# Loading the adjacency of blocks 4 to 15 two blocks at a time in a graph-attention kernel

## The chip, the cores and the metric

The kernel runs on one core of one Trainium2 chip. The metric is the device time of one execution in microseconds; the value of a kernel is the median of its runs. Lower is better.

## The reference, cut to what matters

The reference is one graph-attention layer with a residual and a layer norm. `x` is 4096 x 512, `adj` 4096 x 4096, `W` 512 x 2048 (four heads side by side), all float32.

```python
ht = (h @ W).reshape(N, N_HEADS, N_HIDDEN).transpose(1, 0, 2)
src = einsum('hnd,hd->hn', ht, a_src); dst = einsum('hnd,hd->hn', ht, a_dst)
e = leaky_relu(src[:, :, None] + dst[:, None, :], SLOPE) + adj_mat[None]
att = softmax(e, axis=-1)
h_prime = einsum('hij,hjd->hid', att, ht)
out = layernorm(x + h_prime.mean(axis=0))
```

`adj` holds values up to 1e9, so in each row the largest entry normally outweighs everything else: the attention is then a one at one column, and `h_prime.mean` is the row of `x` at that column times the mean of the heads of `W`. The kernel computes this leading case, tests it with a bound, and has a general branch for blocks in which the test fails. The inputs here stay in the leading case, so the work below is the whole time.

## The kernel before, in words

Rows are taken in 32 blocks of 128: partition p of block ib is row 32p + ib, so consecutive blocks lie side by side in memory on each partition. One block of `adj` is 128 x 4096 float32, 2048 KB, which is 16 KB in a piece on each partition. A core must read all 64 MB of it, besides `x`, `W` and a row of `x` gathered per output row, and it must write 8 MB.

`leading_rows` is one loop over t = 0 to 31, with the order on every engine written out by hand (`manual_schedule`). The engines work on different blocks at the same t:

- **SP** issues all large transfers, in program order. `load_adj` (L119 to L124) loads block t + 5 into one of six buffers; it has to wait until the buffer's last block has been reduced. Blocks from 28 on come in two or four pieces. `load_x` (L127) loads rows of `x` into `hold`, in which part of the rows first hold `W` (`load_w`, L130). After the loop come the stores of `hold` (L338).
- **DVE** reduces block t to maxima of segments of 16, 32 or 64 columns (`segment_maxima`, L180), finds the largest one and its place (`find_segment`, L187 and L189).
- **POOL** fetches that segment out of `adj` again by an indirect DMA (`fetch_segment`, tile `lead`, L200). Two steps later `find_column` (L217, L223) finds the column inside it, and POOL gathers the row of `x` at that column (`gather_rows`, tile `y`, L211). The last block takes another way: `find_column_in_row` (L231) searches the whole row.
- **PE** turns the gathered rows of block t - 3 (`turn`, L238; ACT copies the result, L240), adds the rows of `x` by an identity product (`residual`, L246) and multiplies by the mean of the heads (`products`, L253; halves in L295). In steps 1 to 14 it also turns `W` for the bound (`turn_w`, `head_vector`).
- **ACT and POOL** do the statistics and the scaling of blocks t - 4 and t - 6 (`stats`, `rstd`, `finish`).

The distances are set in the line `COLUMN, PROJECT, STATS, FINISH = 2, 3, 4, 6`. Results are kept in `hold` and stored after the loop, as SP reads its queue in order: first blocks 0 to 7 by four, then 8 to 15 by two, then 16 to 23 by four, then the last eight as they become ready.

A transfer gets one of eight semaphores in turn, and waits for the transfer that had it before.

Of the kernel before, what the change touches and what calls it, by code (L numbers as in the profile page):

```python
# [9 lines left out]
F32 = mybir.dt.float32  # L10
# [10 lines left out]
P = 128  # L21
# [49 lines left out]
def leading_rows(ctx, tc, x, adj, W, a, out, ident, v, n_bad, any_bad):  # L71
# [8 lines left out]
    nc = tc.nc  # L80
    N, D = x.shape
    H = a.shape[0]
    KB, NB = D // P, N // P
    AHEAD = 5
    Q = 4
    PIECES = 4
    LATE = NB - Q
    BEHIND = LATE - Q

    once = ctx.enter_context(tc.tile_pool(name="once", bufs=1))  # L90
    adj_pool = ctx.enter_context(tc.tile_pool(name="adj_pool", bufs=AHEAD + 1))
    y_pool = ctx.enter_context(tc.tile_pool(name="y_pool", bufs=4))
    lead_pool = ctx.enter_context(tc.tile_pool(name="lead_pool", bufs=1))
    LEADS = (8, 8, LAST)
# [3 lines left out]

    adj_rows = adj.rearrange("(p nb) m -> nb p m", nb=NB)
    spans = ((E_EARLY, 0, EARLY), (E, EARLY, NB - LAST), (E_LAST, NB - LAST, NB))  # L100
    adj_segs = {e: adj.rearrange("n (s e) -> (n s) e", e=e) for e, _, _ in spans}
    x_rows = x.rearrange("(p nb) d -> p nb d", nb=NB)
    out_rows = out.rearrange("(p nb) d -> p nb d", nb=NB)
# [1 line left out]


    once.tile([P, 24], F32, name="pad")
    hold = once.tile([P, NB, D], F32, name="hold")
    w_at = NB - KB * H
    w_sum = once.tile([P, KB, D], F32, name="w_sum")  # L110
# [3 lines left out]
    adj_t = {}  # L114

    def pieces(ib):
        return PIECES if ib == NB - 1 else 2 if ib >= LATE else 1

    def load_adj(ib):  # L119
        if 0 <= ib < NB:  # L120
            t = adj_t[ib] = adj_pool.tile([P, N], F32, name="adj_t")
            n = pieces(ib)
            for k in range(n):
                nc.sync.dma_start(t[:, ts(k, N // n)], adj_rows[ib][:, ts(k, N // n)])  # L124

    def load_x(lo, n):
        nc.sync.dma_start(hold[:, ds(lo, n), :], x_rows[:, ds(lo, n), :])  # L127
# [10 lines left out]
    for kb in range(0, KB, 2):  # L138
        load_w(kb, 2)
        load_adj(kb // 2 + 1)  # L140
    for ib in range(KB // 2 + 1, AHEAD):
        load_adj(ib)
    load_x(0, Q)

    make_identity(nc, ident)
# [25 lines left out]
    seg_of, at_of, lead_of, y_t, yt_of, o_ps = {}, {}, {}, {}, {}, {}  # L171
# [13 lines left out]
    def find_segment(ib):  # L185
        seg = seg_of.pop(ib)
        nc.vector.max(out=top[:, ib, :], in_=seg)  # L187
        at = at_of[ib] = small.tile([P, 8], U32, name="at")
        nc.vector.max_index(at, top[:, ib, :], seg)  # L189
        if ib < NB - 1:  # L190
            fetch_segment(ib)
# [17 lines left out]
    def gather_rows(ib, col):  # L209
        y = y_t[ib] = y_pool.tile([P, D], F32, name="y")  # L210
        nc.gpsimd.indirect_dma_start(  # L211
            out=y, out_offset=None, in_=x,
            in_offset=bass.IndirectOffsetOnAxis(ap=col[:, :1], axis=0),
        )

    def find_inner(ib):
        nc.vector.max(out=inner[:, ib, :], in_=lead_of[ib])  # L217

    def find_column(ib):
        if ib < BEHIND:  # L220
            find_inner(ib)
        within = small.tile([P, 8], U32, name="within")
        nc.vector.max_index(within, top[:, ib, :], lead_of[ib])  # L223
        col = small.tile([P, 1], U32, name="col")
        nc.gpsimd.tensor_tensor(col, at_of.pop(ib), within[:, 0:1], op=OP.add)  # L225
        gather_rows(ib, col)
# [7 lines left out]
    def turn(ib):  # L234
        y = y_t.pop(ib)
        tp = psum.tile([P, KB, P], F32, name="tp", bufs=2)
        for kb in range(KB):
            nc.tensor.transpose(tp[:, kb, :], y[:, ds(kb, P, KB)], ident)  # L238
        yt = yt_of[ib] = rows.tile([P, KB, P], F32, name="yt")
        nc.scalar.copy(yt, tp)  # L240

    def residual(ib):
        start = ib not in o_ps
        if start:
            o_ps[ib] = psum.tile([P, D], F32, name="o")
        nc.tensor.matmul(o_ps[ib], ident, hold[:, ib, :], start=start, stop=False)  # L246

    def products(ib, lo=0, hi=KB):
        start = ib not in o_ps
        if start:  # L250
            o_ps[ib] = psum.tile([P, D], F32, name="o")
        for kb in range(lo, hi):
            nc.tensor.matmul(  # L253
                o_ps[ib], yt_of[ib][:, kb, :], w_sum[:, kb, :],
                start=(start and kb == 0), stop=(kb == KB - 1),
            )

    def row_norm(ib):
        sq = rows.tile([P, D], F32, name="sq")
        nc.scalar.activation(sq, hold[:, ib, :], AF.Square, accum_out=xx[:, ib : ib + 1])  # L260

    def put_by(ib):

        if ib == BEHIND:
            o_ps["by"] = adj_pool.tile([P, N // D, D], F32, name="adj_t")
        nc.scalar.copy(o_ps["by"][:, ib - BEHIND, :], o_ps.pop(ib))

    def add_x(engine, ib):
        o = o_ps[ib] = o_ps["by"][:, ib - BEHIND, :]
        engine.tensor_add(o, o, hold[:, ib, :])  # L270

    def stats(ib):
        o, i = o_ps[ib], slice(ib, ib + 1)
        sq = rows.tile([P, D], F32, name="sq")
        nc.scalar.activation(sq, o, AF.Identity, scale=-1.0 / D, accum_out=nm[:, i])  # L275
        sq = rows.tile([P, D], F32, name="sq")
        nc.scalar.activation(sq, o, AF.Square, bias=nm[:, i], accum_out=sd[:, i])  # L277

    def rstd(i):
        nc.gpsimd.tensor_scalar(sd[:, i], sd[:, i], 1.0 / D, EPS, op0=OP.mult, op1=OP.add)  # L280
        nc.gpsimd.tensor_tensor(sd[:, i], sd[:, i], power[:, : i.stop - i.start], op=OP.pow)
        nc.gpsimd.tensor_mul(nm[:, i], nm[:, i], sd[:, i])

    def finish(ib):
        i = slice(ib, ib + 1)
        nc.scalar.activation(hold[:, ib, :], o_ps.pop(ib), AF.Identity, bias=nm[:, i], scale=sd[:, i])  # L286
# [50 lines left out]
    def store(queue, lo, n):  # L337
        queue.dma_start(out_rows[:, ds(lo, n), :], hold[:, ds(lo, n), :])  # L338
# [25 lines left out]
    def head_vector(kb, h, wt):  # L364

        for k in range(KB):
            nc.tensor.matmul(  # L367
                pv[:, kb, h : 2 * H : H], wt[:, k, :], at_d[:, k, h : 2 * H : H],
                start=(k == 0), stop=(k == KB - 1),
            )  # L370
# [57 lines left out]
    vectors = [(kb, h) for kb in range(KB) for h in range(H)]  # L428
    vectors_at = {t: 2 if t < 3 else 1 for t in range(1, 15)}
    COLUMN, PROJECT, STATS, FINISH = 2, 3, 4, 6  # L430

    for t in range(NB):
        if t == NB // 2:
            tc.mark_branch_hint_location("general", engines=HINTED)
        if t in x_at:
            load_x(*x_at[t])
        if t + AHEAD == NB - 1:
            load_x(LATE, Q)
        load_adj(t + AHEAD)
        middle = 1 if t == NB - 1 else 2  # L440
        segment_maxima(t, 0, middle)
        if t >= COLUMN:
            find_column(t - COLUMN)
        segment_maxima(t, middle, PIECES)
        pair = FINISH <= t < BEHIND + FINISH and t % 2 == 0
        if pair:
            rstd(slice(t - FINISH, t - FINISH + 2))
        if t == NB - 1:
            for ib in (BEHIND, BEHIND + 2):
                load_x(ib, 2)  # L450
        find_segment(t)
        if t < 2:
            mean_of_heads(t)
        elif t == 2:
            mean_of_heads(2)
            mean_of_heads(3)
        if t == 0:
            turn_a()
        turned = [(*vectors[0], turn_w(*vectors.pop(0))) for _ in range(vectors_at.get(t, 0))]
        if t == 16:  # L460
            head_norms()
        ib = t - PROJECT
        if t == NB - 1:
            for late in range(LATE, NB):
                row_norm(late)
        if t == NB - 2:
            residual(LATE)
            residual(LATE + 1)
        if ib >= 0:
            turn(ib)  # L470
            if ib > BEHIND:
                products(ib - 1, KB - 1, KB)
            if ib < BEHIND:
                residual(ib)
        for some in turned:
            head_vector(*some)
        if ib >= 0:
            products(ib, 0, KB if ib < BEHIND else KB - 1)
        if t >= BEHIND + STATS:
            put_by(t - STATS)  # L480
        elif t >= STATS:
            stats(t - STATS)
            row_norm(t - STATS)
        if pair:
            finish(t - FINISH)
            finish(t - FINISH + 1)

    for ib in range(BEHIND, LATE):
        row_norm(ib)
    nc.scalar.activation(xx, xx, AF.Sqrt)  # L490
    for ib in range(0, 2 * Q, Q):
        store(nc.sync, ib, Q)
    for ib in range(2 * Q, 4 * Q, 2):
        store(nc.sync, ib, 2)
    for ib in range(4 * Q, BEHIND, Q):
        store(nc.sync, ib, Q)
    add_x(nc.gpsimd, BEHIND)
    find_column(NB - 2)
# [208 lines left out]
```

## Time and profile before

| | us |
|---|---|
| median of 3 runs | 235.0 (234.98 to 235.17) |
| profiled execution, whole | 234.9 |
| its span, first to last instruction | 233.4 |
| around the span | 1.5 |
| DVE busy | 191.3 |
| PE busy | 199.9 |
| queue of SP and ACT transfers, 88.08 MB | 89.1% of 16 engines' span |
| POOL's gathers, 8.84 MB | 9.6% of 16 engines' span |

The span is the profiled execution's own. Engine rows are busy time within it. The two rows on queues give the time that their packets took, divided by the time of all 16 DMA engines.

### The profile page before, as it was taken

To read this page: it belongs to the slowest core of one execution; us is meant where nothing else is said; L and a number is where in the kernel's file an instruction comes from. 1 tells how busy PE (TensorE), PEld (TensorE's weight loads), DVE (VectorE), ACT (ScalarE), POOL (GpSimd) and SP (SyncE) were. 2 spreads that over 40 slices of the span, in tenths; PEclk is the share of its full clock that TensorE was granted. 3 is DMA by queue.
4 is the path that set the end of the run, shared out by engine and by line. 5 is a ranking of instruction groups with operands and counts; after the bars stand their busy time and mean duration, and the time that the engine had idled before them with its cause. 6 is when DMAs were issued, how large, how long until landed. Compare 5 with 4: busy or idle time off the path is not lost.

```text
span 233.4 us, 2484 instructions
## 1 busy us (share of the span) xinstructions
PE 199.9 (86%) x683; PEld 105.3 (45%) x683; DVE 191.3 (82%) x300; ACT 111.8 (48%) x267; POOL 100.7 (43%) x215
## 2 busy tenths in 40 slices
PE   0069995999999999999999779879998977999980
PEld 0034644646565555665645244334443433444460
DVE  0548299689929999999788995999999999998881
ACT  2001223014474757575767455545664644188561
POOL 2020234414524464644543452647464564548300
PEclk9999999579999999999999979999999999999997
DMA  6999999999999999999999999999999999999995
GB/s 237 423 432 428 428 438 426 415 439 436 422 421 437 423 431 425 431 419 428 430 430 428 432 423 432 423 430 421 426 433 420 426 423 426 412 424 420 421 414 213
DMA packets 12257, 97.12 MB, mean 416 GB/s; under 512 B 1992, under 2 KB 2440, under 8 KB 6480
## 3 DMA queue, kind: packets, MB, share of 16 engines
q1 hardware_dynamic: 8640, 88.08, 89.1%
q0 software_dynamic: 3584, 8.84, 9.6%
q8 instruction: 6, 0.10, 0.2%
q14 instruction: 11, 0.09, 0.1%
q10 hardware_dynamic: 16, 0.02, 0.0%
HBM read 88.54 MB, written 8.39 MB: 415 GB/s over the span
## 4 chain that ended last, share of the span: by engine, by line
DMA 64%; DVE 21%; PE 11%; SPq 1%; issue 1%; ACT 0%; DVEq 0%
DMA adj_t<-in_adj_dram 53%; DVE seg L180 17%; DMA hold<-in_x_dram 11%; PE o L253 6%; PE o L295 2%; DVE at L189 1%; PE tp L238 1%; DVE top L187 1%; PE o L246 1%; DVE within L223 1%; SPq L130 1%; PE o L291 0%; SPq L124 0%; DVE inner L217 0%; ACT hold L335 0%
## 5 line engine op out<-in xcount | busy, mean ns | idle before, releaser
L180 DVE TENSOR_REDUCE seg<-adj_t 128x128 f32<-128x2048 f32 (+3 forms) x66 | 145.5, 2208 | 28.5 <-DMA adj_t<-in_adj_dram 28.2
L253 PE MATMUL o<-w_sum,yt 128*128 128x512 f32 x248 | 117.6, 616 | 0.7 <-ACT yt L240 0.7
L253 PEld LDWEIGHTS o<-w_sum,yt 128*128 128x128 f32 x248 | 45.6, 196 | 55.2 <-issue 43.9
L240 ACT COPY yt<-tp 128x512 f32<-128x512 f32 x32 | 18.8, 588 | 43.9 <-PE tp L238 43.8
L200 POOL DMA_INDIRECT lead<-in_adj_dram,row x32 | 32.3, 1008 | 14.6 <-POOL row L196 14.6
L211 POOL DMA_INDIRECT y<-in_x_dram,col x32 | 30.9, 964 | 15.4 <-POOL col L225 15.1
L238 PE MATMUL tp<-ident,y 128*128 128x128 f32 x128 | 22.1, 296 | 10.2 <-DMA y<-in_x_dram,col 10.1
L246 PE MATMUL o<-hold,ident 128*128 128x512 f32 x52 | 28.5, 634 | 1.7 <-DMA hold<-in_x_dram 1.7
L343 PE MATMUL o<-hold,ident 128*128 128x512 f32 x32 | 17.3, 696 | 13.6 <-DMA hold<-in_L_gnn_W_dram 13.6
L238 PEld LDWEIGHTS tp<-ident,y 128*128 128x128 f32 x128 | 18.5, 209 | 22.8 <-issue 20.5
L361 ACT COPY wt<-tp 128x512 f32<-128x512 f32 x16 | 9.2, 587 | 38.2 <-PE tp L359 38.2
L196 POOL TENSOR_TENSOR row<-at,first 128x1 uint32<-128x1 uint32 x32 | 6.1, 190 | 43.6 <-DVE at L189 43.6
L367 PEld LDWEIGHTS pv<-at_d,wt 128*128 128x128 f32 x128 | 17.2, 200 | 7.4 <-ACT wt L361 3.7
L260 ACT ACTIVATE sq<-hold 128x512 f32<-128x512 f32 x32 | 19.8, 620 | 0.0
L225 POOL TENSOR_TENSOR col<-start,within 128x1 uint32<-128x1 uint32 x31 | 5.9, 190 | 32.2 <-DVE within L223 32.2
L286 ACT ACTIVATE hold<-o,nm,sd 128x512 f32<-128x512 f32 x24 | 17.2, 771 | 0.0
L277 ACT ACTIVATE sq<-o,nm 128x512 f32<-128x512 f32 x24 | 16.5, 687 | 0.8
L343 PEld LDWEIGHTS o<-hold,ident 128*128 128x128 f32 x32 | 6.9, 225 | 21.5 <-issue 21.5
L367 PE MATMUL pv<-at_d,wt 128*128 128x2 f32 x128 | 16.0, 249 | 0.6 <-ACT wt L361 0.6
L344 ACT ACTIVATE w_sum<-o 128x512 f32<-128x512 f32 x4 | 2.4, 598 | 27.5 <-PE o L343 27.5
L275 ACT ACTIVATE sq<-o 128x512 f32<-128x512 f32 x24 | 14.5, 606 | 0.0
L187 DVE MAX8 top<-seg 128x8 f32<-128x256 f32 (+2 forms) x32 | 11.6, 362 | 1.1
(86 smaller groups left out, 140.0 us busy)
## 6 DMA issues: line engine op xcount, KB each, us to landing
adj_t<-in_adj_dram SPq DMA_DIRECT2D x28, 2048.0 KB, 30.8
adj_t<-in_adj_dram SPq DMA_DIRECT2D x6, 1024.0 KB, 28.1
hold<-in_L_gnn_W_dram SPq DMA_DIRECT2D x2, 2048.0 KB, 16.4
hold<-in_x_dram SPq DMA_DIRECT2D x2, 2048.0 KB, 37.6
out_dram<-hold SPq DMA_DIRECT2D x4, 1024.0 KB, 16.1
out_dram<-hold SPq DMA_DIRECT2D x7, 512.0 KB, 14.4
hold<-in_x_dram SPq DMA_DIRECT2D x3, 1024.0 KB
adj_t<-in_adj_dram SPq DMA_DIRECT2D x4, 512.0 KB, 19.8
```

Of the source, the lines that this page charges most:

```text
L180: nc.vector.tensor_reduce(seg_of[ib][:, ts(k, N // e // n)], adj_t[ib][:, ts(k, N // n)].rearrange("p (s e) -> p s e", e=e), axis=AX.X, op ...
L200: nc.gpsimd.indirect_dma_start(out=lead, out_offset=None, in_=adj_segs[e], in_offset=bass.IndirectOffsetOnAxis(ap=row[:, :1], axis=0),)
L211: nc.gpsimd.indirect_dma_start(out=y, out_offset=None, in_=x, in_offset=bass.IndirectOffsetOnAxis(ap=col[:, :1], axis=0),)
L238: nc.tensor.transpose(tp[:, kb, :], y[:, ds(kb, P, KB)], ident)
L240: nc.scalar.copy(yt, tp)
L246: nc.tensor.matmul(o_ps[ib], ident, hold[:, ib, :], start=start, stop=False)
L253: nc.tensor.matmul(o_ps[ib], yt_of[ib][:, kb, :], w_sum[:, kb, :], start=(start and kb == 0), stop=(kb == KB - 1),)
L260: nc.scalar.activation(sq, hold[:, ib, :], AF.Square, accum_out=xx[:, ib : ib + 1])
L277: nc.scalar.activation(sq, o, AF.Square, bias=nm[:, i], accum_out=sd[:, i])
L286: nc.scalar.activation(hold[:, ib, :], o_ps.pop(ib), AF.Identity, bias=nm[:, i], scale=sd[:, i])
L343: nc.tensor.matmul(o, ident, hold[:, w_at + kb * H + h, :], start=(h == 0), stop=(h == H - 1))
L367: nc.tensor.matmul(pv[:, kb, h : 2 * H : H], wt[:, k, :], at_d[:, k, h : 2 * H : H], start=(k == 0), stop=(k == KB - 1),)
```

## The change

- The six buffers become one tile `ring` with six slots; block ib has slot ib % 6.
- `load_pair(ib)` issues one transfer for blocks ib and ib + 1 into two neighbouring slots, 32 KB in a piece on each partition. Ahead of the loop it takes the place of `load_adj(4)`, for blocks 4 and 5. Inside the loop it is called at t = 2, 4, 6, 8 and 10, for the pairs 6-7 to 14-15. `load_adj(t + 5)` is called at every t for which t + 5 is not in `PAIRED[2:]`, which is `range(6, 16)`.
- For t = 5 to 18 the steps behind the segment's gather (`find_column`, `turn`, `residual`, `products`, `stats`, `row_norm`, `rstd`, `finish`) are those of t - 1: at t = 5 there are none, and at t = 19 those of 18 and 19 both stand.
- The results of blocks 8 to 15 are stored by two transfers of four blocks, in the place of four transfers of two.

```diff
+    SLOTS = AHEAD + 1
+    PAIRED = range(4, 16)
-    adj_pool = ctx.enter_context(tc.tile_pool(name="adj_pool", bufs=AHEAD + 1))
+    adj_pairs = adj.rearrange("(p nb) m -> p nb m", nb=NB)
+    ring = once.tile([P, SLOTS, N], F32, name="adj_t")
...
+    def load_pair(ib):
+        slot = ib % SLOTS
+        for k in range(2):
+            adj_t[ib + k] = ring[:, slot + k, :]
+        nc.sync.dma_start(ring[:, ds(slot, 2), :], adj_pairs[:, ds(ib, 2), :])
...
-            t = adj_t[ib] = adj_pool.tile([P, N], F32, name="adj_t")
+            t = adj_t[ib] = ring[:, ib % SLOTS, :]
...
-    for ib in range(KB // 2 + 1, AHEAD):
+    for ib in range(KB // 2 + 1, PAIRED[0]):
         load_adj(ib)
+    load_pair(PAIRED[0])
     load_x(0, Q)
...
+    SLACK = range(5, PAIRED[-1] + 4)
     for t in range(NB):
+        steps = [t - 1] if t in SLACK else [t]
+        if t == SLACK[0]:
+            steps = []
+        elif t == SLACK[-1] + 1:
+            steps = [t - 1, t]
...
-        load_adj(t + AHEAD)
+        if t + AHEAD in PAIRED[2:]:
+            if t % 2 == 0:
+                load_pair(t + AHEAD - 1)
+        else:
+            load_adj(t + AHEAD)
         segment_maxima(t, 0, middle)
-        if t >= COLUMN:
-            find_column(t - COLUMN)
+        for u in steps:
+            if u >= COLUMN:
+                find_column(u - COLUMN)
...
-    for ib in range(0, 2 * Q, Q):
-        store(nc.sync, ib, Q)
-    for ib in range(2 * Q, 4 * Q, 2):
-        store(nc.sync, ib, 2)
-    for ib in range(4 * Q, BEHIND, Q):
+    for ib in range(0, BEHIND, Q):
         store(nc.sync, ib, Q)
```

More of the change, by code (lines that the diff above doesn't have):

```diff
@@ L264, in put_by @@
         if ib == BEHIND:
-            o_ps["by"] = adj_pool.tile([P, N // D, D], F32, name="adj_t")
+            o_ps["by"] = ring[:, (ib + 2) % SLOTS, :].rearrange("p (b d) -> p b d", d=D)
         nc.scalar.copy(o_ps["by"][:, ib - BEHIND, :], o_ps.pop(ib))
@@ L438, in leading_rows @@
             load_x(LATE, Q)
-        load_adj(t + AHEAD)
+        if t + AHEAD in PAIRED[2:]:
[3 more added lines that the diff above has]
+            load_adj(t + AHEAD)
         middle = 1 if t == NB - 1 else 2
         segment_maxima(t, 0, middle)
-        if t >= COLUMN:
-            find_column(t - COLUMN)
+        for u in steps:
+            if u >= COLUMN:
+                find_column(u - COLUMN)
         segment_maxima(t, middle, PIECES)
-        pair = FINISH <= t < BEHIND + FINISH and t % 2 == 0
-        if pair:
-            rstd(slice(t - FINISH, t - FINISH + 2))
+        pairs = [u - FINISH for u in steps if FINISH <= u < BEHIND + FINISH and u % 2 == 0]
+        for ib in pairs:
+            rstd(slice(ib, ib + 2))
         if t == NB - 1:
@@ L461, in leading_rows @@
             head_norms()
-        ib = t - PROJECT
         if t == NB - 1:
@@ L468, in leading_rows @@
             residual(LATE + 1)
[L469 to L474, printed above, removed]
+        for u in steps:
+            ib = u - PROJECT
+            if ib >= 0:
+                turn(ib)
+                if ib > BEHIND:
+                    products(ib - 1, KB - 1, KB)
+                if ib < BEHIND:
+                    residual(ib)
+            for some in turned:
+                head_vector(*some)
+            turned = []
+            if ib >= 0:
+                products(ib, 0, KB if ib < BEHIND else KB - 1)
+            if u >= BEHIND + STATS:
+                put_by(u - STATS)
+            elif u >= STATS:
+                stats(u - STATS)
+                row_norm(u - STATS)
         for some in turned:
             head_vector(*some)
[L477 to L486, printed above, removed]
+        for ib in pairs:
+            finish(ib)
+            finish(ib + 1)
     for ib in range(BEHIND, LATE):
```

## The prediction

> **What bounds the kernel now.** I read the page's slices first, then its queues and the chain of waits, then the engines by stage, then the last microseconds by engine. The page (DMA share by slice; queue: packets, MB, share of 16 engines; chain by engine; two rows of the issues):
>
> ```profile
> DMA  6999999999999999999999999999999999999995
> DMA packets 12257, 97.12 MB, mean 416 GB/s; under 512 B 1992, under 2 KB 2440, under 8 KB 6480
> q1 hardware_dynamic: 8640, 88.08, 89.1%
> q0 software_dynamic: 3584, 8.84, 9.6%
> DMA 64%; DVE 21%; PE 11%; SPq 1%; issue 1%; ACT 0%; DVEq 0%
> adj_t<-in_adj_dram SPq DMA_DIRECT2D x28, 2048.0 KB, 30.8
> y<-in_x_dram,col POOLq DMA_INDIRECT x32, 7.8
> ```
>
> The reader is to see that the 16 DMA engines are full from the second slice to the last but one, and that q1 and q0 fill 98.7% of the span between them. A block needs 31 us from issue to landing, about six blocks' worth of queue: a late issue costs nothing as long as data is still queued, and every added byte costs its full time.
>
> By stage (start:end, length, then busy us of PE, PEld, DVE, ACT, POOL, granted clock, DMA share, GB/s):
>
> ```profile
> 70.00:108.00 38.00, 38.00 (x166) 22.88 (x164) 37.14 (x54) 23.65 (x59) 19.81 (x41) 1.00 1.01 427
> 108.00:128.00 20.00, 20.00 (x71) 10.55 (x71) 16.88 (x29) 13.68 (x32) 9.80 (x21) 1.00 1.02 431
> 128.00:160.00 32.00, 26.59 (x72) 11.94 (x71) 28.53 (x45) 15.50 (x39) 16.17 (x36) 0.95 1.01 427
> 160.00:201.00 41.00, 36.65 (x104) 16.16 (x102) 39.78 (x56) 23.10 (x54) 22.90 (x48) 1.00 1.01 425
> ```
>
> DVE and PE are close behind: DVE is full from 70 to 108, PE until 128. PE has 32.00 - 26.59 + 41.00 - 36.65 = 9.8 us to spare between 128 and 201. DMA has none anywhere.
>
> The end, from the timelines of DVE, POOL and PE (start, duration, instruction, idle before it):
>
> ```profile
> 207.19 1.22 DVE L180 TENSOR_REDUCE seg<-adj_t 128x16 f32<-128x1024 f32 x1 [0.23 <-DMA adj_t<-in_adj_dram]
> 209.38 4.42 DVE L231 FIND_INDEX8 col<-top,adj_t 128x8 uint32<-128x4096 f32 x1
> 214.56 0.96 POOL L211 DMA_INDIRECT y<-in_x_dram,col  x1 [0.30 <-issue]
> 221.63 0.72 PE L238 MATMUL tp<-ident,y 128*128 128x128 f32 x4
> ```
>
> The last piece of block 31 lands, DVE searches the row, POOL gathers y of block 31 (trace: landed 221.49) and PE turns it at 221.63. Products, statistics and the last store (issued 228.80, landed 232.40) follow. So the end hangs on the last piece of `adj`, which hangs on everything queued ahead of it.
>
> **What the Trainium skill says.** "DMA: Bandwidth & Descriptors", section on where 436 GB/s comes from: 435 GB/s is the ceiling of the 16 ports. The stages above move 425 to 431, so nothing is left to gain but overhead per packet. Same page, "Two DMAs through the same engine are not ordered": a second write that depends on a first needs a wait on the first one's semaphore ahead of its issue. The trace of before has no such pair of loads. Same page, queues, rings and completion order: each engine alternates between queues at packet granularity. This trace agrees: y took 7.5 to 9.5 us beside 16 KB packets and 6.6 to 6.8 in the three gathers from 179 to 190, beside the 8 KB packets of blocks 28 to 30.
>
> **The change part by part.**
>
> (1) *Block 5 is loaded twice.* `load_pair(4)` ahead of the loop brings blocks 4 and 5. At t = 0 the test asks whether t + 5 = 5 lies in `range(6, 16)`; it does not, so `load_adj(5)` runs as well, into the same slot. The pairs 6-7 to 14-15 have no double. Cost: 2.097 MB more in q1. From the page, 0.891 x 233.4 us for 88.08 MB is 2.36 us per MB, or 4.95 us. From the trace's packet records, 16 KB packets took 613.6 ns in the mean; 128 packets over 16 engines are 8 each, 4.91 us, and one semaphore packet of 9 ns: **+4.92 us**. Nothing hides it: DMA has no gap.
>
> (2) *The wait that this adds.* Both loads write slot 5, so SP should hold the second until the pair lands. By the semaphore packets, block 3 is complete at 32.59 and block 4 at 38.08; the pair then ends near 43. Queued on SP behind the wait are the pairs 6-7 and 8-9 and `x` 4 to 11, issued from 13.56 on before. Those then go out together at 43 to 45, as their slots are long free. In the engines' queue at that moment stands only `x` 0 to 3: 8 packets of 309 ns, 2.5 us. A landing is seen 0.43 us after the slowest engine's semaphore packet (8.22 to 8.65), and the first packet comes 1.0 us after an issue (1.99 against 0.98) and all engines run 1.4 after it. So 1.4 to 1.8 us have to be covered by 2.5 us, less the engines' skew of up to 1.0: a gap of 0 to 0.3 us on the fastest engines, while the slowest set the landings. I take **0**, range 0 to 0.5. Without the wait the sum is the same.
>
> (3) *Pairs.* 12 transfers become 6. Per packet size (median): 4 KB 159 ns, 8 KB 309, 16 KB 611; so about 7 ns per packet are fixed. If 32 KB goes as one packet, each saves 7 ns: 6 x 8 per engine, 0.34 us; net five fewer semaphore packets, 5 x 9 ns = 0.05. **-0.39 us**; the other bound, where packets stay at 16 KB, is -0.05. No packet over 16 KB is in the trace.
>
> (4) *Pair granularity.* The first block of a pair is usable one block (5 us) later, and its slot is refilled only with the second one's. DVE needs 5.66 us per block with 16-column segments (79.52 to 85.18 in the chain), DMA about 5.5. By my walk through the slots DVE is some 4 us late against the data at block 16, and is waiting for DMA again by block 20, since `x` 16 to 23 (5 us) comes in between. At each pair's issue at least 10 us stay queued. **0**, hidden by the queue.
>
> (5) *Steps one block later, 5 to 18.* The same instructions, on PE, ACT, POOL and DVE. PE is full until 128 and works off a backlog, so deferral only reorders it. `x` 0 to 3 lands some 6 us later (40.56 before, near 46), on which the first `residual` already waited 1.5 us; against the shift of (1) that is about 1 us. The double step at 19 puts two blocks together (about 5.4 us of PE each: 0.7 turning, 1.0 residual, 3.7 products), inside the 9.8 us to spare. POOL's queue gets two y gathers in one step (0.96 us each) ahead of a `lead` that has until two steps later; y behind 32 KB packets may take up to 4 x 0.6 = 2.4 us longer, which the later step covers. **0**, bounds 0 to 1.5.
>
> (6) *Stores of 8 to 15 by four.* 512 packets of 4 KB become 256 of 8 KB: 16 per engine x (2 x 159 - 309) = 0.14 us and two semaphore packets, 0.16 us less work. But these stores run from 214.7 to 221.7, exactly beside the gather of y for block 31, which needs four turns per engine; each turn behind 8 KB instead of 4 KB costs up to 150 ns, 0.6 in all, of which PE hides about 0.15. I take **+0.2 us** at the end; bounds 0 and 0.45. The 0.16 us lies behind other stores and is not on the chain.
>
> Sum on the profiled execution: 234.9 + 4.92 - 0.39 + 0.2 = 239.6 us. The median of the runs shown is 235.0, 0.1 above that execution; I leave that out. Against 235.0 this is 2.0% slower.
>
> **The rivals.** A change within 0.2% (0.5 us) is about what a measurement of this kernel can tell from none.
>
> *A, the forecast:* one block more in a full queue. 239.0 (no late gather, lower rate per packet) to 240.3 (16 KB packets, a gap of 0.3). Chance 0.72.
>
> *B, a second wait on top:* SP's hold, or y gathers behind 32 KB packets followed by the double step, lets DMA run dry or makes PE late at 201. For it: PE is full until 128 and at 0.83 of its clock between 40 and 70. Against it: 9.8 us to spare and 10 us of queue. A gap of one landing round trip (1.8 us) or PE late by 2 gives 241.4 to 242. Chance 0.18.
>
> *C, larger packets pay more than sizes up to 16 KB show,* so that the slow engines (2 us behind the fast ones from block 20 on) catch up: 238.5 to 239. Chance 0.05.
>
> *D, not slower:* the second load of block 5 never takes engine time, because it is not in the program or the pairs win it back. To win it back, each of 48 packets per engine would have to save 102 ns of 1222, 29.3 GB/s per engine, where the best row has 26.7. Its point: q1 at 88.08 MB instead of 90.18. Then 234.9 - 0.39 + 0.2 = 234.7, at best 234.3. Chance 0.05.
>
> **How the numbers follow.** The likeliest is A, 239.6. The range 238.8 to 241.3 leaves out D, half of B and half of C, together somewhat under 0.2. Slower by over 0.2%: A, B and C, 0.95. D splits into 0.03 faster and 0.02 the same.
>
> **What would show it.** q1 at 90.18 MB and HBM read 2.1 MB up, q1's time up by 4.4 to 4.8 us; seven fewer transfers on SP. SP's second load of block 5 waiting for the pair until about 43, block 5's reduction starting near 52 (47.62 before). 32 KB packets would confirm (3). DVE waiting for DMA again about block 20; the landing of the last piece 4.5 us later; y of block 31 taking 7.0 to 7.5 us (6.93 before). I am wrong if q1's bytes are unchanged, if the DMA share dips between 40 and 50, or if PE at 201 works on older blocks.

## The result and the profile after

The changed kernel takes 255.5 us in the median (254.5 to 256.3) against 235.1 us before: a ratio of 1.087, 95% interval 1.083 to 1.090. It is slower, as forecast, but by 20.4 us and not by 4.6. The profiled execution took 254.5 us, with a span of 252.9. In the experiments below, one run each of two kernels fell into a slower state (over 1.5% above the fastest run of its kernel) and is left out of the median.

First the page of the changed kernel (DMA share and GB/s by slice; queue: packets, MB, share; chain by engine; issues: number, KB each, median us to landing):

```profile
DMA  6999999999999999999999999999999999993134
GB/s 253 429 438 426 429 455 394 424 444 418 444 441 422 437 427 425 437 394 430 423 435 428 425 436 430 415 437 428 421 418 427 422 417 427 426 409 118 47 144 194
q1 hardware_dynamic: 7632, 90.18, 84.0%
DMA 37%; PE 34%; issue 10%; POOL 10%; ACT 4%; DVE 3%; POOLq 0%; SPq 0%; DVEq 0%
adj_t<-in_adj_dram SPq DMA_DIRECT2D x6, 4096.0 KB, 26.0
y<-in_x_dram,col POOLq DMA_INDIRECT x32, 8.3
```

Two things are as forecast. q1 moves 90.18 MB, so block 5 is loaded twice. And no slice from the second to the 36th falls below 394 GB/s, so SP's hold on the second load (it ends at 43.14 us, in the seventh slice) opens no gap worth naming. What was not forecast stands at the right end. The DMA engines, which in the kernel before are full up to the last slice but one, stand idle for most of the last four slices (118, 47, 144, 194 GB/s; a slice is 6.3 us). The chain says the same: DMA held 64% of it and now 37%, PE 11% and now 34%. **DMA no longer sets the end.**

By stage (start:end, length, then busy us of PE, PEld, DVE, ACT, POOL, granted clock, DMA share, GB/s):

```profile
40.00:70.00 30.00, 24.00 (x85) 14.26 (x86) 18.11 (x22) 7.27 (x18) 6.73 (x14) 0.74 1.02 431
70.00:108.00 38.00, 29.46 (x105) 17.09 (x105) 31.28 (x46) 15.17 (x36) 15.73 (x35) 0.87 0.99 424
108.00:128.00 20.00, 19.33 (x82) 11.32 (x81) 19.49 (x30) 11.91 (x28) 10.38 (x22) 1.00 1.01 426
128.00:160.00 32.00, 29.40 (x93) 14.87 (x91) 23.27 (x44) 18.76 (x46) 15.79 (x33) 0.95 1.01 429
```

From 70 to 108, where both were full before (PE 38.00, DVE 37.14), PE is now busy for 29.46 us and DVE for 31.28. This is in the middle of a stage in which DMA is still full. So both engines idle while data flows.

The end, from the timelines of DVE and POOL (start, duration, instruction, idle before it):

```profile
222.99 1.20 DVE L190 TENSOR_REDUCE seg<-adj_t 128x16 f32<-128x1024 f32 x1
229.87 4.42 DVE L241 FIND_INDEX8 col<-top,adj_t 128x8 uint32<-128x4096 f32 x1
235.05 0.96 POOL L221 DMA_INDIRECT y<-in_x_dram,col  x1 [0.58 <-PE o L301]
```

By the updates of its semaphore the last piece of `adj` has landed at 209.57, only 2.40 us later than before (207.17). DVE begins its block at 222.99, without waiting for anything: it comes late itself. Before, it began that block at 202.84 and waited for the last piece.

**Where it was lost.** Taking the start of PE's turn (`turn`) of each block, after less before: block 3 is 14.2 us later, block 4 18.5, block 7 22.2, block 10 22.2, block 17 25.4, block 24 20.3, block 31 20.5. By 110 us 22 us are lost. Another 3 come by block 17 (around the head norms, see below), 5 are made up by block 24, and nothing after that. Blocks 3 and 7 in the timelines of the changed kernel (DVE, POOL, PE; start, duration, instruction, idle before it):

```profile
62.78 2.29 DVE L190 TENSOR_REDUCE seg<-adj_t 128x128 f32<-128x2048 f32 x1 [4.34 <-DMA adj_t<-in_adj_dram]
66.08 0.96 POOL L221 DMA_INDIRECT y<-in_x_dram,col  x1 [0.52 <-POOL col L235]
77.49 1.10 PE L248 MATMUL tp<-ident,y 128*128 128x128 f32 x4 [6.21 <-DMA y<-in_x_dram,col]
...
94.21 0.96 POOL L221 DMA_INDIRECT y<-in_x_dram,col  x1 [0.27 <-POOL col L235]
109.89 0.72 PE L248 MATMUL tp<-ident,y 128*128 128x128 f32 x4 [0.67 <-DMA y<-in_x_dram,col]
```

And block 3 in the kernel before (POOL, PE):

```profile
50.92 0.96 POOL L211 DMA_INDIRECT y<-in_x_dram,col  x1 [0.51 <-POOL col L225]
63.30 0.65 PE L238 MATMUL tp<-ident,y 128*128 128x128 f32 x4
```

The first line of the changed kernel is the reduction of block 6, behind which the column search of block 3 now stands. Before, that search stood behind block 5, which began at 47.62, and the gather of y was issued at 50.92, 3.30 us later. Now it is issued at 66.08, again 3.30 us after 62.78. The 15.16 us between the two issues are therefore 5.69 for the later step (block 6 began 5.69 us after block 5 before) and 9.47 because block 6 itself comes later (the second load and the pairs). The gather then takes 11.28 us in the place of 8.21, and 4.17 us are absorbed, as y used to land at 59.13 and was turned at 63.30: 15.16 + 3.07 - 4.17 = 14.06, measured 14.19. For block 7: issue 16.08 later, gather 15.54 us in the place of 7.48, 2.12 absorbed: 22.0, measured 22.2.

What DVE, PE and POOL wait for in the changed kernel (us in all, times, longest), and below it the same of the kernel before:

```profile
DVE seg L190 <- DMA adj_t<-in_adj_dram: 33.1, 7, 8.5
DVE inner L227 <- DMA lead<-in_adj_dram,row: 9.3, 4, 3.3
DVE n L389 <- PE px L387: 7.4, 1, 7.4
PE tp L248 <- DMA y<-in_x_dram,col: 20.1, 9, 6.2
POOL sd L290 <- ACT sq L287: 32.1, 8, 6.3
```

```profile
DVE seg L180 <- DMA adj_t<-in_adj_dram: 28.2, 11, 8.7
DVE n L379 <- PE px L377: 1.1, 1, 1.1
PE tp L238 <- DMA y<-in_x_dram,col: 10.1, 10, 2.7
POOL sd L280 <- ACT sq L277: 8.0, 5, 3.3
```

PE waits twice as long for y (10.1 us before). POOL waits 32.1 us for statistics (8.0 before); PE's lateness reaches POOL by them, and the next `lead` is queued behind them. DVE does the same work (190.7 us busy, 191.3 before), but its waits for `adj`, `lead` and the head norms grew by 4.9, 10.1 (with 1.0 at L233, which was 0.2) and 6.3 us. That is 21.3 us, beside 19.5 us of span.

### The profile page after: what moved, and what is told of

It reads as the page before. It is cut to its first block, busy times and chain, and to the rows that moved or that the text cites. A ratio compares the mean times of both kernels' runs of the same rounds, so it can differ in the third digit from the quotient of the medians.

```text
span 252.9 us, 2464 instructions
## 1 busy us (share of the span) xinstructions
PE 205.5 (81%) x683; PEld 109.1 (43%) x683; DVE 190.7 (75%) x300; ACT 112.0 (44%) x267; POOL 100.0 (40%) x215
## 3 DMA queue, kind: packets, MB, share of 16 engines
q1 hardware_dynamic: 7632, 90.18, 84.0%
## 4 chain that ended last, share of the span: by engine, by line
DMA 37%; PE 34%; issue 10%; POOL 10%; ACT 4%; DVE 3%; POOLq 0%; SPq 0%; DVEq 0%
PE o L263 21%; DMA adj_t<-in_adj_dram 20%; DMA y<-in_x_dram,col 17%; PE o L256 4%; PE tp L248 4%; POOL lead L210 4%; POOL y L221 2%; DVE seg L190 2%; PE pv L377 2%; POOL sd L291 1%; PE o L305 1%; ACT sq L287 1%; ACT sq L285 1%; ACT yt L250 1%; POOL start L217 1%
## 5 line engine op out<-in xcount | busy, mean ns | idle before, releaser
L263 PE MATMUL o<-w_sum,yt 128*128 128x512 f32 x248 | 121.5, 634 | 0.8 <-ACT yt L250 0.7
L263 PEld LDWEIGHTS o<-w_sum,yt 128*128 128x128 f32 x248 | 47.3, 202 | 58.3 <-issue 46.7
L248 PE MATMUL tp<-ident,y 128*128 128x128 f32 x128 | 22.5, 302 | 20.3 <-DMA y<-in_x_dram,col 20.1
L248 PEld LDWEIGHTS tp<-ident,y 128*128 128x128 f32 x128 | 19.6, 208 | 31.9 <-issue 29.8
L353 PE MATMUL o<-hold,ident 128*128 128x512 f32 x32 | 16.8, 680 | 13.4 <-DMA hold<-in_L_gnn_W_dram 13.4
L377 PEld LDWEIGHTS pv<-at_d,wt 128*128 128x128 f32 x128 | 18.1, 209 | 8.3 <-issue 4.4
L377 PE MATMUL pv<-at_d,wt 128*128 128x2 f32 x128 | 16.9, 256 | 1.3 <-ACT wt L371 1.3
L290 POOL TENSOR_SCALAR sd<-sd 128x2 f32<-128x2 f32 (+1 forms) x13 | 2.5, 189 | 32.4 <-ACT sq L287 32.1
## 6 DMA issues: line engine op xcount, KB each, us to landing
hold<-in_x_dram SPq DMA_DIRECT2D x3, 1024.0 KB, 12.9
```

Source lines behind the costliest of these rows:

```text
L263: nc.tensor.matmul(o_ps[ib], yt_of[ib][:, kb, :], w_sum[:, kb, :], start=(start and kb == 0), stop=(kb == KB - 1),)
L353: nc.tensor.matmul(o, ident, hold[:, w_at + kb * H + h, :], start=(h == 0), stop=(h == H - 1))
L377: nc.tensor.matmul(pv[:, kb, h : 2 * H : H], wt[:, k, :], at_d[:, k, h : 2 * H : H], start=(k == 0), stop=(k == KB - 1),)
```

## The experiments

Beside each ratio stands its 95% interval; the kernel before took 235.1 to 235.2 us in each comparison.

**Which part costs what.** The theories: S, the later steps hold most of the loss; D, the second load does; G, the pairs do, with the gathers that run beside them.

*The change without the second load of block 5.*

```diff
-        if t + AHEAD in PAIRED[2:]:
-            if t % 2 == 0:
+        if t + AHEAD in PAIRED[1:]:
+            if t > 0 and t % 2 == 0:
```

> The changed kernel without the second load of block 5 at t = 0 (the pairs, the later steps and the stores stay). Theory S (PE is starved): the later steps and the pairs make y of block 3 late, PE stands idle, and it has no time to make that up. Then taking the second load out gives back its 4.9 us of DMA and about half of PE's gap: 244 to 249 us, and PE still waits for y between 45 and 75. Rival D (the second load and SP's hold are nearly the whole): 234.5 to 237. Rival G (gathers are slow behind 32 KB packets): 248 to 251, as only the DMA time of one block goes.

Measured: 250.5 us, 1.064 (1.061 to 1.067). The second load is worth 5.0 us here, the predicted size (4.92).

*The kernel before, with block 5 loaded a second time at t = 0.*

```diff
+        if t == 0:
+            t5 = adj_t[5]
+            nc.sync.dma_start(t5, adj_rows[5])
```

> The kernel before with the second load of block 5 alone, issued at t = 0 behind the first. Theory S: single blocks keep coming and the steps stand where they were; the block costs its DMA time of 4.9 us and little more: 239.5 to 242. Rival D: 248 or more. Rival G: 239.5 to 242, as S.

Measured: 243.6 us, 1.037 (1.035 to 1.039), 8.5 us. Here SP's hold does open a gap, from the page (by slice, of 6.0 us):

```profile
GB/s 253 430 431 432 435 422 426 262 377 431 427 422 425 430 424 428 432 428 419 432 438 420 431 428 430 431 427 423 423 432 425 420 424 426 411 425 419 426 394 197
```

Two slices fall to 262 and 377 GB/s, which makes about 2.9 us. In this kernel `x` 0 to 3 is queued ahead of block 5, so nothing is left in the queue while SP waits. In the changed kernel it stands behind the pair and fills just that gap.

*The change without the later steps.* The second load stays.

```diff
-    SLACK = range(5, PAIRED[-1] + 4)
+    SLACK = range(0, 0)
...
-        if t == SLACK[0]:
-            steps = []
-        elif t == SLACK[-1] + 1:
-            steps = [t - 1, t]
```

> The changed kernel with the steps where they were before (no step one block later); the second load, the pairs and the stores stay. Theory S: y of block 3 is gathered at t = 5 (near 55) and not at t = 6 (66): PE loses some 5 us and not 14, 242 to 247. Rival D: 253 to 256. Rival G: the gathers stay slow and now have a block less to come, so it is as slow or slower, 255 to 262.

Measured: 249.0 us, 1.063 (1.056 to 1.070). The later steps are worth 6.5 us in the changed kernel.

*Both taken out: pairs and stores are left.* The two edits above together.

> The changed kernel without the second load and with the steps in their places: pairs and stores by four alone. Theory S: 236 to 242, what is left is the wait for the second block of a pair. Rival D: 234.5 to 236. Rival G: 245 or more.

Measured: 243.5 us, 1.035 (1.033 to 1.037), +8.4 us. So every part costs: pairs with stores 8.4, later steps 7.0 (250.5 - 243.5), second load 5.0. These are the steps of one row of kernels, so they make up the 20.4 us by construction. Taken out in the other order the second load is worth 5.5 (249.0 - 243.5) and the later steps 6.5, so the parts nearly add. Only the first of the four results lies in a range given for it (G's). None of the three theories alone holds.

*Single loads, with the later steps and the stores.*

```diff
-    load_pair(PAIRED[0])
+    load_adj(PAIRED[0])
...
-        if t + AHEAD in PAIRED[2:]:
-            if t % 2 == 0:
-                load_pair(t + AHEAD - 1)
-        else:
-            load_adj(t + AHEAD)
+        load_adj(t + AHEAD)
```

> The changed kernel with single loads throughout (no pairs, no second load): the steps of 5 to 18 one block later, and stores by four, are all that is left. Theory S: y of block 3 is gathered one block later (5.7 us), which PE has not in store at that time, and POOL's rstd waits for late statistics ahead of a lead; most of a block is lost and part of it made up from the 9.8 us to spare: 238 to 242. The prediction's reading (PE works off a backlog, later steps cost nothing): 234.8 to 235.5.

Measured: 241.7 us, 1.029 (1.026 to 1.032), +6.6 us. This is in S's range, and the prediction's reading fell. The later steps cost about the same with no pairs about. PE turns blocks 3 and 4 2.1 us later than before. The step of block 5, from the timelines of POOL and PE of this kernel:

```profile
72.25 0.96 POOL L221 DMA_INDIRECT y<-in_x_dram,col  x1 [0.55 <-POOL col L235]
81.06 1.10 PE L248 MATMUL tp<-ident,y 128*128 128x128 f32 x4 [3.23 <-DMA y<-in_x_dram,col]
```

Before, y of block 5 was issued at 63.48, landed at 72.55 and was turned at 75.52, with PE busy until then. Issued 8.77 us later (a step is that long here, as block 8 begins 10 us after block 7), it lands at 80.92, and PE idles for 3.23 us and is 5.54 us late. A gather of ordinary length is enough for that.

*The kernel before, with the stores of 8 to 15 by four.*

```diff
-    for ib in range(0, 2 * Q, Q):
-        store(nc.sync, ib, Q)
-    for ib in range(2 * Q, 4 * Q, 2):
-        store(nc.sync, ib, 2)
-    for ib in range(4 * Q, BEHIND, Q):
+    for ib in range(0, BEHIND, Q):
         store(nc.sync, ib, Q)
```

> The kernel before with the results of blocks 8 to 15 stored by four blocks, nothing else. The prediction's step: y of block 31 comes up to 0.45 us later and 0.16 us of work goes: 235.1 to 235.5. Rival: nothing to be measured, 234.9 to 235.1.

Measured: 235.4 us, 1.0015 (1.0002 to 1.0027): the predicted +0.2. In its profiled execution y of block 31 took 7.54 us, against 6.93. That this makes the 0.2 us is not shown.

**What it is in the pairs.**

*Pairs and stores, with slots 32 bytes longer, so that each partition's 32 KB no longer lies in one piece and goes as two packets of 16 KB.*

```diff
-    ring = once.tile([P, SLOTS, N], F32, name="adj_t")
+    ring = once.tile([P, SLOTS, N + 8], F32, name="adj_t")
...
```

> Pairs and stores by four alone, steps in place, no second load, x behind the pair; each slot of the ring is 32 bytes longer, so that a pair is still one transfer of 4 MB but its packets should be 16 KB. Theory S in two parts: y lands in 8 us again, PE's waits from 80 to 108 go, the loss between 40 and 60 stays: 238.5 to 241. Theory G: 235 to 236. Theory P: 243 to 244.

Measured: 239.6 us, 1.018 (1.016 to 1.020). 3.9 us less than with 32 KB packets.

*The changed kernel with one edit of that kind: its slots are 512 bytes longer (`N + 128`), so that the pairs go in packets of 16 KB.*

> The changed kernel whole, with the second load, the later steps and the stores; only its slots are 512 bytes longer, so that the pairs go in 16 KB packets. If the costs add up, the packets' 4 to 6 us go: 249.5 to 251.5. If the later steps already cover the slow gathers: 254 to 256.

Measured: 251.1 us, 1.068 (1.061 to 1.074), 4.4 us less than the changed kernel. Landing of y, then of `lead`, in the window 60 to 112 us, of the changed kernel, and below of this one (us from DMA to landing):

```profile
DMA to landing us min/median/max: 8.2/13.6/15.7
DMA to landing us min/median/max: 6.2/12.5/14.5
```

```profile
DMA to landing us min/median/max: 7.2/7.5/7.9
DMA to landing us min/median/max: 5.9/6.3/7.0
```

The 7.5 rests on two gathers, as the landing of the others isn't told. By the packet records, the last packet of y comes 7.1 us after the issue in the median of all eight gathers of this window, against 12.0 in the changed kernel. Same steps, same transfers on SP: only the packets are halved, and the gathers are back near the times of before (8.1 and 6.2 to the landing in that window). So it is the packets of 32 KB on SP's queue that slow the gathers on POOL's. The page's median over the whole span, 8.3 against 7.8, hides this, as only about a third of the gathers run beside the pairs.

*Pairs and stores, with `x` 0 to 3 ahead of the first pair.* It tests whether the late `x` is what delays PE.

```diff
-    load_pair(PAIRED[0])
     load_x(0, Q)
+    load_pair(PAIRED[0])
```

> Pairs and stores by four alone, with the steps in place and no second load, as the run that took 243.5 us; x of blocks 0 to 3 is now loaded ahead of the first pair instead of behind it. Theory S, by now in two parts: PE loses about 5.6 us between 40 and 60 because x of 0 to 3 lands behind 4 MB, and about 4.5 us between 80 and 108 because y comes late behind 32 KB packets. This takes the first part out: 237.5 to 240. Theory G (only the gathers behind 32 KB packets): 243 to 244, no change. Theory P (it is the pair's granularity, blocks that come two at a time): 242 to 244.

Measured: 243.1 us, 1.035 (1.032 to 1.038), 0.4 less than without, which the intervals don't tell from none. My reading that `x` cost several microseconds fell.

*That edit with packets of 16 KB.*

> Both at once: pairs with 16 KB packets, x of blocks 0 to 3 ahead of the first pair, steps in place, no second load, stores by four. Theory S in two parts: 234.8 to 236.5, as nothing is left of either part. Theory P: 240 or more, since blocks still come two at a time.

Measured: 238.9 us, 1.016 (1.015 to 1.018). Its 16 KB packets took 624 ns in the mean, against 613.6 before: 4096 packets on 16 engines make 2.7 us. So the longer slots seem to have a price of their own, and the result lies between the two theories.

*The same with slots 512 bytes longer (`N + 128`).*

> As the run with x ahead and 16 KB packets that took 238.9 us, but each slot of the ring is 512 bytes longer instead of 32. In that run the 16 KB packets took 624 ns in the mean against 614 before, and 256 such packets per engine make 2.7 us. Theory L (the odd slot length costs it, pairs as such cost nothing): 235 to 236.5, packets at 612 to 616 ns. Theory P (blocks two at a time cost the rest): 238.5 to 239.5 with packets at 614.

Measured: 237.4 us, 1.009 (1.007 to 1.010), packets at 613.9 ns. So 1.5 us of the kernel before it came from the slots' length. Against the kernel with 32 KB packets and `x` ahead (243.1) the packet size itself is worth 5.7 us. What stays, 2.25 us, is between the ranges of L and P. It is the pairs' granularity, with the stores' 0.2 and whatever `x` ahead of the pair does.

*Pairs from block 8 on, slots 512 bytes longer, no later steps.* Theory F tied the cost of granularity to the start of the kernel.

```diff
-    PAIRED = range(4, 16)
+    PAIRED = range(8, 16)
...
```

> Pairs of blocks 8 to 15 in 16 KB packets (slots 512 bytes longer), blocks 0 to 7 single as before, x where it was, steps in place, stores by four. Theory F (the first pair at 4-5 holds back the column of block 2 and starves PE near 50; later pairs are free): 235.1 to 235.9. Theory P (blocks two at a time cost time anywhere): 236.5 to 238.

Measured: 238.5 us, 1.015 (1.012 to 1.019), +3.3 us, above both ranges. The timelines of DVE, POOL and PE at the first pair:

```profile
74.61 2.29 DVE L189 TENSOR_REDUCE seg<-adj_t 128x128 f32<-128x2048 f32 x1 [9.29 <-DMA adj_t<-in_adj_dram]
77.93 0.97 POOL L220 DMA_INDIRECT y<-in_x_dram,col  x1 [0.54 <-POOL col L234]
86.95 0.89 PE L247 MATMUL tp<-ident,y 128*128 128x128 f32 x3 [5.60 <-DMA y<-in_x_dram,col]
```

Block 8 begins 5.46 us later (69.15 before), because the whole pair must land first. The column search of block 6 stands behind it on DVE, so y of block 6 is issued 5.45 us later (72.48 before), and PE idles for 5.60 and turns it 5.33 us later. F fell: a first pair at block 8 holds up the column search and the gather behind it, as one at block 4 does (with pairs and stores alone, y of block 2 is issued 3.9 us later than before).

*The kernel before, with blocks 16 to 23 in pairs of 32 KB packets and nothing else,* where PE had time to spare: a version that might have been faster. Of the edit against the changed kernel one line is shown; the second load, the later steps and the stores by four are out.

```diff
-    PAIRED = range(4, 16)
+    PAIRED = range(16, 24)
...
```

> The kernel before with pairs for blocks 16 to 23 only, in 32 KB packets, steps in place, stores as before, x as before. If slow gathers matter only where PE has nothing to spare, this costs nothing, and DMA saves 4 pairs x (8 x 9 + 9) ns = 0.3 us: 234.5 to 235.3. If gathers behind 32 KB packets cost everywhere as at blocks 4 to 15 (8 us for 6 pairs): 238 to 241.

Measured: 243.3 us, 1.033 (1.031 to 1.036), +8.2 us and above both ranges. DVE's waits on `lead` in this kernel:

```profile
DVE inner L226 <- DMA lead<-in_adj_dram,row: 6.9, 4, 3.6
```

Block 16 begins 5.4 us later (121.26 against 115.83), and y takes up to 13.4 and `lead` up to 12.9 us beside the pairs. The time that PE had to spare there did not help: DVE has only 4.7 us to spare between 128 and 201 (32.00 - 28.53 + 41.00 - 39.78 in the kernel before), and ends 8.4 us late at block 31.

**What it is in the later steps.** A theory was that POOL passes the delay on: `rstd` waits there for late statistics with the next `lead` behind it. Another was the head norms at t = 16, for which DVE waits 7.4 us.

*Single loads, later steps, with `rstd` moved behind `find_segment`, so behind POOL's `lead`.*

```diff
-        for ib in pairs:
-            rstd(slice(ib, ib + 2))
...
         find_segment(t)
+        for ib in pairs:
+            rstd(slice(ib, ib + 2))
```

> The later steps with single loads and stores by four, which took 241.65 us; now POOL gets rstd behind the fetch of the segment and not ahead of it. Theory Q (POOL waits in rstd for late statistics while the next lead stands behind it, and DVE then waits for lead: 9 us): 236.5 to 239. Theory S alone (PE lost the time at blocks 3 to 7 and has nowhere to make it up): 241 to 242.

Measured: 239.9 us, 1.020 (1.014 to 1.025), 1.7 less than the same without the move. The runs spread from 238.4 to 241.9, so this gain is not well fixed, and the median lies in neither range.

*Single loads, with the later steps from 12 to 18 only.*

```diff
-    SLACK = range(5, PAIRED[-1] + 4)
+    SLACK = range(12, PAIRED[-1] + 4)
```

> The later steps with single loads and stores by four, but from t = 12 to 18 and not from 5; the double step at 19 stays. Theory C (the catching up at 19 costs it: two y gathers ahead of a lead, two blocks at once on PE and POOL): 239.5 to 242. Theory B (the start at 5 costs it, where PE has no backlog): 235 to 237.

Measured: 238.8 us, 1.016 (1.014 to 1.019), +3.6 us, against 6.6 from t = 5, and between the two ranges. Three of the 6.6 us belong to the start at 5; the rest comes with a start at 12 too.

*The changed kernel, with DVE's part of the head norms at t = 22.*

```diff
...
         if t == 16:
-            head_norms()
+            norms_ps = head_norms()
+        if t == 22:
+            head_norms_rest(norms_ps)
```

> The changed kernel whole; the head norms at t = 16 are split: DVE's squares and PE's product stay at 16, DVE's reductions of the product come at 22, so that DVE doesn't wait for a late PE (7.4 us in the changed kernel). If DVE's waits add up to the loss: 249 to 252. If PE alone sets the end (it is as late either way): 254 to 256.

Measured: 253.0 us, 1.077 (1.075 to 1.079), 2.5 less, and between the two ranges. DVE's wait moved on:

```profile
DVE both L395 <- ACT n L393: 5.3, 1, 5.3
```

The 7.4 us at PE became 5.3 us at ACT, whose queue is late too.

*That one, with `rstd` moved as above.*

> As the run with the head norms split, and POOL gets rstd behind the fetch of the segment. If POOL's wait for late statistics (32 us in the changed kernel) holds up leads: 2 to 5 us below the run with the split alone. If the leads are late because of the 32 KB packets and the two y gathers ahead of them: within 1 us of it.

Measured: 253.7 us, 1.076 (1.072 to 1.081): no further gain. *Pairs and stores alone, with both moves:*

> Pairs of 32 KB and stores by four alone (no second load, steps in place, 243.5 us), with the head norms split and rstd behind the fetch. DVE waited 10.7 us for lead there and 1.2 at the head norms. If these leads are slow in the DMA queue itself, behind 32 KB packets: 242.5 to 244, hardly less. If POOL held them: 238 to 241.

Measured: 242.4 us, 1.031 (1.029 to 1.033), 1.1 less than without them. So POOL's hold and the head norms are ways by which the delay reaches DVE, but not its source. Taking one away gives back between nothing and 2.5 us, and leaves the rest of the delay to the others.

No kernel tried beats the kernel before.

## Why the prediction was right and wrong

**Right in size: (1), the bytes.** The second load was put at 4.92 us and measured 5.0. The way was only half as told. Early on, data is what DVE waits for: without the second load block 6 begins at 57.88 and not at 62.78, 4.90 us earlier. But the prediction let the bytes act at the end, on the last piece of `adj`, and neither kernel waits for that piece. That PE and DVE passed the early 4.9 us on almost unchanged is partly luck: the same load cost 5.5 us with the steps in place, and 8.5 alone.

**Right: (2), the hold.** SP's second load went out at 43.14, as soon as the pair was there, and `x` 0 to 3 covered the gap. The kernel with the second load alone shows what happens without that cover. **(3), the rate,** was about right: a 32 KB packet took 1213 ns in the median, 9 ns less than two of 16 KB, predicted 7. **(6), the stores,** measured +0.2 by themselves, as predicted. In the changed kernel the term has no place: with the DMA engines mostly idle, its y of block 31 landed in 3.3 us (6.93 before). Rival D is out: q1 is at 90.18 MB.

**Wrong: (5), the later steps: 0 in the sum, 1.5 at most, measured 6.5 to 7.0.** The step said "PE is full until 128 and works off a backlog, so deferral only reorders it". PE was full, but its backlog was less than one step. In the trace of before, y of blocks 3, 7, 11 and 14 landed 4.2, 2.1, 3.9 and 0.9 us before PE turned them, and from block 3 on no y was more than 5.0 us ahead; a step in that stretch is about 5.7 us or more. So moving the gather by a step made PE wait, as the kernel with the later steps alone shows at block 5. As long as PE stayed full, it could not win that back.

**Wrong: (4), granularity: 0, measured about 2 to 3** (2.25 with pairs from 4 and `x` ahead, 3.3 with pairs from 8, each less the stores' 0.2). It was argued that DVE is behind its data by block 16 anyway. The step overlooked what is queued behind the waiting reduction: DVE's column search for the block two before, and with it that block's gather and PE. With pairs from 8, DVE is 5.5 us late at block 8 and 5.8 at block 15, PE 5.3 at block 6 and 6.8 at block 14: neither made it up in that stage.

**Wrong: the gathers beside 32 KB packets, in (5): 2.4 us for y, covered by the later step, measured up to 8 us for y.** The same was not asked of `lead` at all, which went from 6.2 to 12.5 us in the median, and which DVE waits for. The packet size costs 4.4 us in the changed kernel and 5.7 with pairs and stores alone and `x` ahead. The prediction's 2.4 us counted only the turns of y's own four packets on each engine, and for these it was near: in y of block 7, first and last packet start 2.8 us further apart than before. But the first one starts 9.1 us after the issue, against 4.05 before. And a `lead` is only one packet on each engine, and still came 6.3 us later. What a gather waits for ahead of its first packet, no run here shows.

**Wrong: the reserve.** Rival B named the right kind of thing, late gathers with PE behind, but priced it at 2 us beyond A, because of the 9.8 us that PE has to spare between 128 and 201. PE's spare time was the wrong one to count: in the same two stages DVE has 4.7 us. Once the head norms and the late `lead` had made DVE late, the remaining time could not bring it back: block 17 begins 16.6 us later than before, block 31 20.2.

The forecast that DVE waits again for DMA by block 20, and that the last piece lands 4.5 us later, fell with it. The piece came 2.4 us later. By my estimate the rest is work not yet asked for: at 20 us late and 5.6 us per block, the gathers of some 3.5 blocks come after it, each 0.70 us of DMA time (9.6% of 233.4 us for 32 blocks), 2.5 us together, where 2.1 are missing.

**Open:** the granted clock fell to 0.74 between 40 and 70 (0.83 before), and to 0.87 after that. What share of PE's lateness comes from the clock, and whether the clock fell because PE idled, no run here separates. It is not needed for the later steps' loss: in the profiled execution of the later steps alone the clock was 0.961 over the span, against 0.965 before, and 5.8 us were lost (240.7 against 234.9). Nor is it shown how the 3.6 us of the later steps from 12 on divide between that start and the double step at 19.

## What to carry to other kernels

Before deferring a step or making transfers coarser, measure how long each input lies ready before its consumer takes it: here that margin, and not the consumer's busy share, said what a delay costs. When a load is made later, follow what is queued behind the instruction that waits for it, and count spare time on the engine that sets the pace at the end. Here larger packets in one queue were paid for by short transfers in another, so compare their landing times in that stage, and not by a median over the whole span.

## What the runs showed of the hardware

- Beside 32 KB packets in SP's queue, the gathers of POOL's queue took 13.6 us (y) and 12.5 us (`lead`) in the median, beside 16 KB packets 7.5 (of two gathers) and 6.3, while a 32 KB packet (1213 ns in the median) moved its bytes only 0.7% faster than two of 16 KB (611 each).
- With destination slots 32 bytes longer than 16 KB the 16 KB packets took 624 ns in the mean; 512 bytes longer, 613.9; not longer (the kernel before), 613.6.
- SP's hold for one landing cost no DMA time where 2.5 us of other transfers were queued, and about 2.9 us where none were.
